# Rounding by conversion to int16, a clip moved to VectorE, separate priorities for the first and last batches, and a last batch without softmax transfers

## The chip, the cores and the metric

The kernel runs on one core of a Trainium2 chip. Its time is the device time of one execution in microseconds (us), and lower is better. The core has five engines that run side by side and meet at semaphores: TensorE (PE, matmuls, results in PSUM), VectorE (DVE), ScalarE (ACT), GpSimd (POOL) and SyncE (SP), whose queue issues all DMA transfers of this kernel.

## The reference

For each of 32 batches (x and context are 128 x 512 in f32): cross-attention over 8 heads, then a feed-forward network whose weights are ternary and whose activations are rounded to 8 bits per token.

```python
x = x + xattn(layernorm(x), ctx)      # 8 heads of 16 channels, rope on 8 of them, softmax over 512 keys
x = x + ffn(layernorm(x))

def act_quant(x):                     # per token
    scale = 128 / clip(max(abs(x)), 1e-5)
    return clip(round(x * scale), -128, 127) / scale

def weight_quant(w):                  # one scale for a whole matrix
    scale = 1 / clip(mean(abs(w)), 1e-5)
    return clip(round(w * scale), -1, 1) / scale

def ffn(x):                           # 512 -> 2048 -> 512
    gate, up = bitlinear(x, w_gate), bitlinear(x, w_up)
    return einsum(act_quant(fwht(silu(gate) * up)), weight_quant(w_down))
```

`fwht` is a Walsh-Hadamard transform over the 2048 channels.

## The kernel before

Every batch passes through some forty stages. Each stage is a Python generator (`s_load`, `s_a`, ..., `s_dn`) that loops over the batches and yields what it needs next: a buffer of a ring (`get`), an event of another stage (`on`), or an engine for a stated time. The class `Plan` runs all generators against a model of the engines and so writes down one fixed order of instructions for each engine. It takes the step that can start first by its model; among steps of the same engine that could start within `eps` of it, the one with the lowest rank goes first. A rank is the stage's number in `CFG` plus `T` times the batch index, as the stage last gave it with `at`; a stage without an `at` (the weight stages `w`, `w1` to `w4`, `const`, `init`) keeps its number. On TensorE `stick` is taken off the rank of a step whose matmul shape ("full", "half" or "cols") is that of the step before. `pen` keeps a step that two engines could do on the first named.

Attention of a batch: `s_load` fetches x and context; `s_a`, `s_a2`, `s_a3` normalise, project and apply rope, and write `xd` to DRAM; `s_st` reads it back as `qs` and `ks`. The 16 steps of `s_mpe` write scores to `pS` (two PSUM banks, one such buffer), `s_mdve` takes their row maxima `M` on VectorE (L657), `s_mfin` sends them back through DRAM into `qs`. `s_epe` repeats the scores into `pT` (also one buffer), `s_eact` takes the exponential on ScalarE (L725), and `s_eav` multiplies by the values, to which columns of ones are appended, so that `pav` holds the sums of the softmax too. `pS` and `pT` matmuls use half of the array's rows each ("half"). `s_u` copies `pav` to `U` (L769) and writes it to DRAM as `ud`. `s_o` reads from there the sums `sc` and the values `N`, inverts the sums (`rc`, L800), writes them out as `rd`, reads them back spread over 128 partitions as `RB`, and multiplies (L812). A matmul with `WOT` (L821) and an addition (L825) make `x1`.

Feed-forward: `s_o2` normalises `x1`, rounds it by adding 12582912 on ScalarE into a PSUM bank `w` (L854), subtracts that and clips at 127 on VectorE (L857) into `xq`, and a DMA transposes it to `xqT`. Gate and up projections (L880), silu (L910), product (L935), four rounds of butterflies (`s_bf`, L964, on GpSimd or VectorE) and two Hadamard matmuls (`s_hm`) fill `y`, 128 x 2048 in f32, of which there is one buffer. `s_am` finds each token's maximum, `s_q` scales (L1099), and `s_q1` and `s_q2` round and clip in two ScalarE passes over each half:

```python
nc.scalar.activation(y, y, AF.Identity, bias=MAG)                                  # s_q1, L1109
nc.scalar.activation(s["yq"][:, w], s["y"][:, w], AF.Relu, bias=MAG7, scale=-1.0)  # s_q2, L1123
nc.tensor.matmul(ps, s["yq"][:, j, :], WDQ[:, j, :], ...)                          # s_dn, L1141, 16 of them
nc.tensor.matmul(ps, NEG, CS, start=False, stop=True)                              # s_dn, L1142
```

The second pass holds 127 - y, so the down projection comes out as 127 times a column sum of the weights less what is wanted; one more matmul with `NEG` and the column sums `CS` takes that off, and `yc` carries the minus sign. `CS` is made once, in `s_w4`, with 16 matmuls (L418), four small VectorE steps and a transfer. `s_dn` then scales, adds `x1` (L1147) and writes the batch out.

At the start the three weight matrices are read in twelve pieces (`s_w`), summed by absolute value (`s_w1`), scaled, rounded, clipped and converted (`s_w2` to `s_w4`). The first gate matmul waits for all of them (`wr`, 2). The ring `pf` holds three PSUM banks that almost all full-array matmuls share, and `x1` has four buffers.

Of the kernel before, what the change touches and what calls it, by code (L numbers as in the profile page):

```python
# [13 lines left out]
F8 = mybir.dt.float8e4  # L14
AF = mybir.ActivationFunctionType
# [5 lines left out]
MAGIC = 12582912.0  # L21
# [4 lines left out]
    "a": 17040.0,  # L26
    "a2": 9587.6,
    "a3": 24145.2,
    "am": 15370.4,
    "bf": 32443.0,  # L30
    "const": -13702.6,
    "dn": -12954.6,
    "eact": -26357.5,
    "eav": 10024.8,
    "epe": -25661.6,
    "gact": 12255.9,
    "gpe": 25689.6,
    "hi": 17693.4,
    "hm": -13331.7,
    "init": -13147.7,  # L40
    "lo": 14260.1,
    "load": -14103.3,
    "mdve": -26910.2,
    "mfin": -15116.6,
    "mpe": -17532.8,
    "o": -16894.5,
    "o2": -35355.2,
    "q": 9579.7,
    "q1": 31393.3,
    "q2": 30321.2,  # L50
    "st": -39068.5,
    "u": 12892.7,
    "udve": -12899.7,
    "upe": 40468.8,
    "v": 41001.5,
    "w": 11036.2,
    "w1": 23901.9,
    "w2": 38371.3,
    "w3": 34207.9,
    "w4": 33907.2,  # L60
    "yv": -12466.7,
    "zt": 12210.4,
    "T": 69.4,
    "eps": 0.025,
    "pen": 8.4,
    "stick": 7462.1,
    "epspe": 0.214,
# [5 lines left out]
    "xq": 1, "xqT": 2, "pf": 3, "z0": 2, "z1": 1, "hl": 2, "y": 1, "yq": 2, "ot": 1,  # L73
# [3 lines left out]
class Plan:  # L77

# [16 lines left out]
    def __init__(self, nc, rings, cfg):  # L95
# [12 lines left out]
        self.locked = False  # L108
        self.tail = 0
# [11 lines left out]
    def step(self, t):  # L121
        self.now = max(t[1], t[7] + self.LAT[t[6]]) if t[6] else t[1]
        while True:
# [10 lines left out]
            t[0] = self.cfg[t[4]] + self.cfg["T"] * r[1]  # L134
# [45 lines left out]
    def run(self):  # L180
        for t in list(self.tasks):
            self.step(t)
        while True:
# [4 lines left out]
            for t in self.tasks:  # L188
# [5 lines left out]
                elif isinstance(r[0], tuple):  # L194
                    f = [(self.start(t, e), e, d) for e, d in zip(*r[:2])]
                    pen = self.cfg["pen"] if t[5] < self.tail else 0.0
# [29 lines left out]
def xattn_ffn(  # L226
# [41 lines left out]
    MAG7 = const.tile([128, 1], F32, name="MAG7")  # L268
    nc.vector.memset(MAG7, MAGIC + 127.0)
# [10 lines left out]
    CW = const.tile([128, 388], F32, name="CW")  # L280
    WQ, WK, WVT, BRP, MASK = CW[:, 0:128], CW[:, 128:256], CW[:, 256:384], CW[:, 384:386], CW[:, 386:387]
    NEGC = CW[:, 387:388]
    CM = const.tile([128, 386], F32, name="CM")
    EYE, WOT, HADF, BVO = CM[:, 0:128], CM[:, 128:256], CM[:, 256:384], CM[:, 384:386]
    ROPE = const.tile([128, 2, T], F32, name="ROPE")
    COS, SIN = ROPE[:, 0, :], ROPE[:, 1, :]
    HAD = const.tile([128, 128], FR, name="HAD")
    BO = const.tile([128, 1], F32, name="BO")
# [8 lines left out]
    ob = const.tile([128, 1], BF, name="ob")  # L297
    nc.vector.memset(ob, 1.0)
    NEG = const.tile([2, 128], BF, name="NEG")
    CS = const.tile([2, 512], BF, name="CS")  # L300

    p = Plan(nc, RINGS, CFG)
    p.tail = NB - 2
    st = [dict() for _ in range(NB)]
    NU = 2 * NB
    EARLY = 6

    def s_const():
# [6 lines left out]
        nc.scalar.copy(HAD, HADF)  # L315
        p.mark("had")
# [9 lines left out]
    def s_init():  # L326
        yield "on", "cw"
        yield "dve", 0.2
        nc.vector.tensor_scalar(NEG, ones[0:2, :], NEGC[0:2], None, ALU.mult)
        z = zeros[:, :, None].to_broadcast([128, 2, T])  # L330
        for i in range(4):
            yield ("dve", "pool"), (1.13, 1.4), "port"
            E[p.eng].tensor_scalar(kss[i], z, MASK, None, ALU.add)
            p.mark("ks", i)
# [69 lines left out]
    def s_w4():  # L404
# [8 lines left out]
        yield "get", "y"  # L413
        yield "get", "pf"
        yield "pe", 3.5
        pc = ps_f.tile([128, 512], F32, name="pf")
        for j in range(NI):
            nc.tensor.matmul(pc[0:1, :], ob, WDQ[:, j, :], start=(j == 0), stop=(j == NI - 1))  # L418
        yield "dve", 0.6
        w = fp.tile([128, 2048], F32, name="y")  # L420
        ca, cb = w[0:1, 0:512], w[0:1, 512:1024].bitcast(BF).rearrange("p (a f) -> p a f", a=2)
        nc.vector.tensor_scalar(ca, pc[0:1, :], 1.0 / 64.0, MAGIC, ALU.mult, ALU.add)
        yield "dve", 0.6, "port"
# [794 lines left out]
```

## Time and profile before

| | |
|---|---|
| three runs | 1440.73, 1450.44 (median), 1453.01 us |
| profiled execution | 1449.79 us, of which the span is 1447.9 us |
| mean granted TensorE clock | 0.95 |
| busy share of the span | TensorE 94%, VectorE 81%, ScalarE 82%, GpSimd 68% |
| first and last `U` copy (L769) | 82.5 and 1365.3 us |
| first and last `ot` (L1147) | 278.7 and 1444.3 us |
| DMA queue of the kernel | 137588 packets, 213.84 MB, 50.4% of 16 engines' span |

The span runs from the first to the last instruction. A busy share is the time in which an engine had an instruction at work; matmuls are pipelined, their ends are modelled, and a busy TensorE need not be at its peak. "L12" is line 12 of the kernel; names such as `pf<-hi,HAD` are the tile written and the tiles read. An arrow in the idle column names what ended the idle time.

### The profile page before, as it was taken

What the parts mean: (1) busy time and instruction counts of PE and PEld (TensorE: products, weight loads), DVE (VectorE), ACT (ScalarE), POOL (GpSimd) and SP (SyncE); (2) the same over time, 40 slices, a digit from 0 to 9 for tenths busy, and PEclk for the clock granted to TensorE, in tenths of its full rate; (3) what the DMA queues carried; (4) which work ended last, traced back from release to release, by engine and by line L of the source; (5) the groups of instructions that cost most, each with busy time, mean ns of one, the idle gap of its engine ahead of it and who ended that gap; (6) DMA issues with size and microseconds to landing.
All of it is one profiled execution on the core that took longest, in us unless ns stands there. A gap on an engine that the chain in (4) does not pass through costs nothing.

```text
span 1447.9 us, 21862 instructions
## 1 busy us (share of the span) xinstructions
PE 1354.9 (94%) x7448; PEld 529.9 (37%) x7448; DVE 1173.9 (81%) x1755; ACT 1192.3 (82%) x1575; POOL 990.2 (68%) x778
## 2 busy tenths in 40 slices
PE   3797799999999999999999999999999999999965
PEld 1222233333334343333334433334333434433322
DVE  2975878888888888888888888888889888886565
ACT  5778977888988888888888888888888888888743
POOL 3112319987777878877777787887777777777830
PEclk7567999999999999999999999999999999999986
DMA  8948745454456565555445556555544555321100
GB/s 284 294 145 270 220 110 159 145 145 117 150 157 173 166 175 166 155 151 149 118 153 161 170 170 174 167 153 147 144 129 149 163 170 155 94 72 43 41 26 14
DMA packets 137699, 215.23 MB, mean 149 GB/s; under 512 B 37618, under 2 KB 39924, under 8 KB 136564
## 3 DMA queue, kind: packets, MB, share of 16 engines
q1 hardware_dynamic: 137588, 213.84, 50.4%
q8 instruction: 59, 0.97, 0.3%
q14 instruction: 52, 0.43, 0.1%
HBM read 107.35 MB, written 93.85 MB: 139 GB/s over the span
## 4 chain that ended last, share of the span: by engine, by line
PE 77%; POOL 7%; DVE 6%; ACT 5%; DMA 3%; issue 2%; SPq 0%; POOLq 0%; ACTq 0%; DVEq 0%
PE pav L746 16%; PE pf L880 13%; PE pT L712 13%; PE pS L642 9%; PE pf L1141 8%; POOL z L964 4%; PE pf L472 4%; PE pf L984 4%; PE pf L1023 3%; ACT P L725 2%; PE pf L821 2%; PE pf L552 2%; PE pf L1024 2%; DVE M L657 2%; POOL N L812 1%
## 5 line engine op out<-in xcount | busy, mean ns | idle before, releaser
L964 POOL TENSOR_TENSOR z<-z 128x512 f32<-128x512 f32 x489 | 616.7, 1283 | 103.0 <-DVE z L935 60.7
L657 DVE TENSOR_REDUCE M<-pS 128x2 f32<-128x1024 f32 x488 | 595.1, 1219 | 90.6 <-PE pS L642 89.1
L725 ACT ACTIVATE P<-pT 128x1024 f32<-128x1024 f32 x512 | 523.0, 1022 | 145.6 <-PE pT L712 144.0
L746 PE MATMUL pav<-P,va 128*32 128x512 f32 x2048 | 281.8, 623 | 0.0
L712 PE MATMUL pT<-qs,ks 50*128 50x512 f32 x1024 | 260.1, 504 | 20.8 <-ACT P L725 18.7
L642 PE MATMUL pS<-ks,qs 48*128 48x512 f32 x976 | 227.5, 457 | 12.3 <-DVE M L657 7.5
L712 PEld LDWEIGHTS pT<-qs,ks 50*128 50x128 f32 x1024 | 97.8, 187 | 242.2 <-ACT P L725 144.0
L448 POOL TENSOR_TENSOR arstd<-arstd,MHALF 128x1 f32<-128x1 f32 x32 | 18.5, 579 | 195.6 <-DVE arstd L445 160.5
L880 PEld LDWEIGHTS <-xqT 128*128 128x128 bf16 x1024 | 91.8, 99 | 155.3 <-issue 83.2
L1099 POOL TENSOR_TENSOR y<-y,YB 128x1024 f32<-128x1024 f32 x60 | 140.9, 2369 | 9.0 <-ACT YB L1085 9.0
L1141 PE MATMUL pf<-WDQ,yq 128*128 128x512 fp8e4 x512 | 127.9, 396 | 16.3 <-ACT yq L1123 16.3
L1051 DVE TENSOR_REDUCE ya<-y 128x128 f32<-128x1024 f32 x64 | 127.3, 1989 | 12.9 <-ACT y L1038 12.6
L642 PEld LDWEIGHTS pS<-ks,qs 48*128 48x128 f32 x976 | 95.9, 190 | 112.8 <-issue 43.5
L880 PE MATMUL pf<-WGQ,xqT 128*128 128x512 fp8e4 x512 | 131.4, 382 | 0.9 <-DVE ot L1147 0.5
L880 PE MATMUL pf<-WUQ,xqT 128*128 128x512 fp8e4 x512 | 126.8, 381 | 0.5 <-DVE X L525 0.2
L935 DVE TENSOR_TENSOR z<-z,pf 128x512 f32<-128x512 f32 x128 | 84.3, 675 | 17.2 <-PE pf L880 13.7
L996 ACT CAST hi<-pf 128x512 fp32r<-128x512 f32 x128 | 74.1, 586 | 26.8 <-PE pf L984 26.7
L910 ACT ACTIVATE z<-pf,tk 128x512 f32<-128x512 f32 x128 | 84.1, 684 | 8.0 <-PE pf L880 4.7
L1007 DVE TENSOR_TENSOR lo<-pf,hi 128x512 fp32r<-128x512 f32 x128 | 85.5, 675 | 3.0 <-ACT hi L996 3.0
L1141 PEld LDWEIGHTS <-yq 128*128 128x128 bf16 x512 | 46.7, 101 | 99.3 <-ACT yq L1123 27.4
L984 PE MATMUL pf<-CM,z 128*128 128x128 f32 x512 | 82.2, 285 | 0.8 <-DVE z L964 0.4
L1038 ACT COPY y<-pf 128x512 f32<-128x512 f32 x128 | 71.7, 584 | 9.5 <-PE pf L1024 9.4
(118 smaller groups left out, 1780.0 us busy)
## 6 DMA issues: line engine op xcount, KB each, us to landing
xd<-X SPq DMA_DIRECT2D x128, 512.0 KB
qs<-xd SPq DMA_DIRECT2D x128, 192.0 KB
ks<-xd SPq DMA_DIRECT2D x128, 192.0 KB
ud<-U SPq DMA_DIRECT2D x64, 256.0 KB
xt<-x SPq DMA_DIRECT2D x32, 256.0 KB
ct<-cx SPq DMA_DIRECT2D x32, 256.0 KB
RR<-R SPq DMA_DIRECT2D x64, 128.0 KB
N<-ud SPq DMA_DIRECT2D x32, 256.0 KB
```

Of the source, the lines that this page charges most:

```text
L642: nc.tensor.matmul(ps[e], qs[w, t, bass.ts(qt, 128)], ks[w, t, :], start=True, stop=True)
L657: nc.vector.tensor_reduce(m, ps[2], AX.X, ALU.max)
L712: nc.tensor.matmul(ps[:, e], ks[w, t, bass.ts(kt, 128)], qs[w, t, :], start=True, stop=True)
L725: nc.scalar.activation(P, TQ[u, n], AF.Exp, scale=0.25)
L746: nc.tensor.matmul(av[32 * h : 32 * h + 32, :], va[:, kt, 4 * hf + h, :], P[:, e], start=(kt == 0), stop=(kt == 3),)
L880: nc.tensor.matmul(ps, xqT[:, k, :], W[:, k, bass.ts(c, 512)], start=(k == 0), stop=(k == 3))
L964: E[p.eng].tensor_tensor(ix(dv, k), ix(av, 0), ix(av, 1), o)
L984: nc.tensor.transpose(ps[:, i, :], st[b]["z"][:, bass.ts(4 * c + i, 128)], EYE)
L1007: nc.vector.tensor_tensor(t, F.pop(("z", b, c)), F["hi", b, c].bitcast(F32), ALU.subtract)
L1051: nc.vector.tensor_reduce(ya[:, h], s["y"][:, 8 * h : 8 * h + 8].rearrange("p j t -> p t j"), AX.X, ALU.max, apply_absolute_value=True,)
L1099: E[p.eng].tensor_tensor(y, y, st[b]["YB"].to_broadcast([128, 8, 128]), ALU.mult)
L1141: nc.tensor.matmul(ps, s["yq"][:, j, :], WDQ[:, j, :], start=(j == 0), stop=False)
```

## The change

x is rounded by ScalarE's conversion to int16 (`xi`, in SBUF) and clipped at 127 by VectorE into `xq`. y is converted to int16 by ScalarE (`yi`, a new buffer; `y` is released after that) and clipped into `yq` by VectorE. `yq` now holds y itself: the correction matmul, `NEG`, `CS` and the making of the column sums are gone, and the first down projection waits for `wr`, 2. Each stage has three numbers in `CFG`, the one with `.h` for batches below 4 and the one with `.z` for the last four; all numbers and the planner's constants have other values. In the last batch (`SHORT`) the division of the softmax is done on VectorE by a reciprocal of `pav`, a shuffle of partitions and a product, the output projection by two matmuls with a spread copy of the weight (`WOZ`), and the transpose of `xq` by matmuls with a unit matrix and a copy. Parts are left out below; most lines of `CFG` among them.

```diff
 CFG = {
...
-    "epe": -25661.6,
-    "gpe": 25689.6,
-    "load": -14103.3,
-    "mpe": -17532.8,
-    "o": -16894.5,
-    "o2": -35355.2,
-    "w": 11036.2,
-    "T": 69.4,
-    "eps": 0.025,
-    "pen": 8.4,
-    "stick": 7462.1,
...
+    "epe": -29108.4,
+    "gpe": 54531.7,
+    "gpe.z": 1547.0,
+    "load": 44634.2,
+    "load.h": -38799.1,
+    "mpe": -16692.5,
+    "mpe.h": -40256.1,
+    "mpe.z": -21815.0,
+    "o": -21945.0,
+    "o.z": 51451.2,
+    "o2.z": -36890.7,
+    "w": 57939.8,
+    "T": 848.2,
+    "eps": 0.104,
+    "pen": 30.7,
+    "stick": 4180.0,
...
-    "xq": 1, "xqT": 2, "pf": 3, "z0": 2, "z1": 1, "hl": 2, "y": 1, "yq": 2, "ot": 1,
+    "xq": 1, "xqT": 2, "pf": 3, "z0": 2, "z1": 1, "hl": 2, "y": 1, "yq": 2, "yi": 1, "ot": 1,
...
-            t[0] = self.cfg[t[4]] + self.cfg["T"] * r[1]
+            part = ".h" if r[1] < self.head else ".z" if r[1] >= self.tail else ""
+            t[0] = self.cfg.get(t[4] + part, self.cfg[t[4]]) + self.cfg["T"] * r[1]
...
-                    pen = self.cfg["pen"] if t[5] < self.tail else 0.0
+                    pen = self.cfg["pen"] if t[5] < self.tail + 2 else 0.0
...
+    WOZ = CM[:, 386:642]
...
+    EYEB = const.tile([128, 128], BF, name="EYEB")
...
-    ob = const.tile([128, 1], BF, name="ob")
-    nc.vector.memset(ob, 1.0)
-    NEG = const.tile([2, 128], BF, name="NEG")
-    CS = const.tile([2, 512], BF, name="CS")
...
-    p.tail = NB - 2
+    p.head = 4
+    p.tail = NB - 4
...
+    SHORT = (NB - 1,)
+    SWAP = [i % 16 + 16 for i in range(32)]
...
+        yield "act", 0.2
+        nc.scalar.copy(EYEB, EYE)
...
-        yield "get", "y"
-        yield "get", "pf"
-        yield "pe", 3.5
-        pc = ps_f.tile([128, 512], F32, name="pf")
-        for j in range(NI):
-            nc.tensor.matmul(pc[0:1, :], ob, WDQ[:, j, :], start=(j == 0), stop=(j == NI - 1))
...
-        nc.sync.dma_start(out=CS, in_=cb)
-        p.now = p.done
-        p.put("y")
-        p.mark("cs")
...
+            if b in SHORT:
+                yield "get", "RB"
+                yield "dve", 0.7
+                av = TQ.pop(u)
+                U = op.tile([128, T], F32, name="U", bufs=2)
+                nc.vector.reciprocal(U, av)
+                yield "dve", 0.8
+                RB = op.tile([128, T], F32, name="RB")
+                nc.vector.stream_shuffle(RB, U, SWAP)
+                yield "dve", 0.68
+                nc.vector.tensor_tensor(U, av, RB, ALU.mult)
+                p.put("pa")
+                p.put("RB")
+                st[b]["U", hf] = U
+                p.mark("ud", u)
+                continue
...
+    def add_x1(b, po, xr):
+        yield "dve", 0.66
+        x1 = x1p.tile([128, T], F32, name="x1")
+        nc.vector.scalar_tensor_tensor(x1, po, BO, xr, ALU.add, ALU.add)
+        p.put("pf")
+        p.put("xr")
+        st[b]["x1"] = x1
+        p.mark("x1", b)
...
+            if b in SHORT:
+                yield "dma", 0.73, 0.45, 1.2
+                xr = op.tile([128, T], F32, name="xr")
+                nc.sync.dma_start(out=xr, in_=x[b])
+                p.marks["xr", b] = p.done
+                if b == 0:
+                    yield "on", "bo"
+                yield "on", "ud", 2 * b + 1
+                yield "get", "x1"
+                yield "on", "xr", b
+                yield "get", "pf"
+                yield "pe", 1.88
+                po = ps_f.tile([128, 512], F32, name="pf")
+                for hf in range(2):
+                    nc.tensor.matmul(po, WOZ[:, bass.ts(hf, 128)], s["U", hf], start=(hf == 0), stop=(hf == 1))
+                p.put("U", 2)
+                yield from add_x1(b, po, xr)
+                continue
...
-            yield "get", "pf"
-            yield "act", 0.75
-            w = ps_f.tile([128, 512], F32, name="pf")
-            nc.scalar.activation(w, l2, AF.Identity, bias=MAG, scale=sx)
-            yield "dve", 0.6
+            yield "act", 0.65
+            xi = xp.tile([128, T], I16, name="xi", bufs=1)
+            nc.scalar.activation(xi, l2, AF.Identity, scale=sx)
+            p.put("l2")
+            yield "dve", 0.35, "port"
             xq = xp.tile([128, T], BF, name="xq", bufs=1)
-            nc.vector.tensor_scalar(xq, w, -MAGIC, 127.0, ALU.add, ALU.min)
-            p.put("pf")
-            p.put("l2")
+            nc.vector.tensor_scalar(xq, xi, 127.0, None, ALU.min)
             yield "get", "xqT"
-            yield "dma", 0.5, 1.23
-            xqT = fp.tile([128, 4, 128], BF, name="xqT", bufs=2)
+            if b in SHORT:
+                yield "get", "pf"
+                yield "pe", 0.4
+                pt = ps_f.tile([128, 4, 128], F32, name="pf")
+                for k in range(4):
+                    nc.tensor.matmul(pt[:, k, :], xq[:, bass.ts(k, 128)], EYEB, start=True, stop=True)
+                p.put("xq")
+                yield "act", 0.48
+                xqT = fp.tile([128, 4, 128], BF, name="xqT", bufs=2)
+                nc.scalar.copy(xqT, pt)
+                p.put("pf")
+            else:
+                yield "dma", 0.5, 1.23
+                xqT = fp.tile([128, 4, 128], BF, name="xqT", bufs=2)
+                nc.sync.dma_start_transpose(out=xqT, in_=xq)
+                p.now = p.done
+                p.put("xq")
             s["xqT"] = xqT
...
-            nc.vector.tensor_scalar(yc, yc, SW[:, 2:3], -1.0, ALU.mult, ALU.mult)
+            nc.vector.tensor_scalar(yc, yc, SW[:, 2:3], None, ALU.mult)
...
+                if hf == 0:
+                    yield "get", "yi"
                 yield "act", 1.05
-                y = st[b]["y"][:, 8 * hf : 8 * hf + 8]
-                nc.scalar.activation(y, y, AF.Identity, bias=MAG)
+                if hf == 0:
+                    st[b]["yi"] = fp.tile([128, NI, 128], I16, name="yi", bufs=RINGS["yi"])
+                w = slice(8 * hf, 8 * hf + 8)
+                nc.scalar.copy(st[b]["yi"][:, w], st[b]["y"][:, w])
                 p.mark("q1", b, hf)
+            p.put("y")
 
     def s_q2():
         for b in range(NB):
@@ -1116,13 +1221,13 @@
             yield "get", "yq"
             for hf in range(2):
                 yield "on", "q1", b, hf
-                yield "act", 1.05
+                yield "dve", 0.45, "port"
                 if hf == 0:
                     s["yq"] = fp.tile([128, NI, 128], BF, name="yq", bufs=RINGS["yq"])
                 w = slice(8 * hf, 8 * hf + 8)
-                nc.scalar.activation(s["yq"][:, w], s["y"][:, w], AF.Relu, bias=MAG7, scale=-1.0)
+                nc.vector.tensor_scalar(s["yq"][:, w], s["yi"][:, w], 127.0, None, ALU.min)
                 p.mark("yq", b, hf)
-            p.put("y")
+            p.put("yi")
...
-                yield "on", "cs"
+                yield "on", "wr", 2
             yield "get", "pf"
             ps = ps_f.tile([128, 512], F32, name="pf")
             for g in range(2):
                 if g:
                     yield "on", "yq", b, 1
-                yield "pe", 1.73 + 0.22 * g
+                yield "pe", 1.73
                 for j in range(8 * g, 8 * g + 8):
-                    nc.tensor.matmul(ps, s["yq"][:, j, :], WDQ[:, j, :], start=(j == 0), stop=False)
-            nc.tensor.matmul(ps, NEG, CS, start=False, stop=True)
+                    nc.tensor.matmul(ps, s["yq"][:, j, :], WDQ[:, j, :], start=(j == 0), stop=(j == NI - 1))
...
+    woz = np.zeros((2, 4, 32, 128), f)
+    woz[:, :, 0:16] = a["L0_xattn_Wo"].T.reshape(2, 4, 16, 128)
+    woz = woz.transpose(1, 2, 0, 3).reshape(128, 256)
+    r["cm"] = np.concatenate([np.eye(128, dtype=f), a["L0_xattn_Wo"].T, h, bvo, woz], 1)
```

## The prediction

> **What bounds the kernel now.** I read four views, in this order: the windows (busy time of each engine by stage), TensorE's timeline over one steady batch, the groups of instructions of ScalarE and VectorE, and the chain that ended last, for its end.
>
> The windows first. I cut them at events of the trace: the last weight conversion ends by 187 us, the first `ot` is at 278.7, the last `pS` matmul at 1316.6, the last `U` copy at 1365.3. The columns are length, busy us of TensorE, its weight load, VectorE, ScalarE and GpSimd, then granted clock, DMA share and GB/s.
>
> ```profile
> core 0: us, PE busy (x) PEld busy (x) DVE busy (x) ACT busy (x) POOL busy (x), PEclk, DMA share, GB/s
> 0.00:100.00 100.00, 66.72 (x254) 25.32 (x258) 61.21 (x105) 67.84 (x85) 26.35 (x28) 0.61 0.75 247
> 100.00:187.00 87.00, 69.30 (x352) 21.43 (x344) 61.48 (x88) 80.01 (x89) 20.77 (x19) 0.83 0.78 234
> 187.00:279.00 92.00, 89.18 (x486) 33.13 (x484) 69.65 (x102) 70.91 (x92) 62.70 (x51) 0.98 0.46 129
> 279.00:1317.00 1038.00, 1034.55 (x5945) 409.92 (x5942) 903.98 (x1331) 895.97 (x1205) 815.18 (x635) 1.00 0.52 149
> 1317.00:1366.00 49.00, 44.52 (x237) 17.35 (x236) 23.93 (x46) 41.39 (x57) 46.10 (x35) 1.00 0.12 37
> 1366.00:1448.00 82.00, 50.61 (x188) 22.79 (x186) 53.62 (x86) 36.22 (x51) 19.09 (x13) 0.78 0.09 28
> ```
>
> From 279 to 1317 TensorE is idle 3.5 us of 1038, at clock 1.00. Busy matmul time alone proves little, so I looked at how they follow each other:
>
> ```profile
> 803.20 0.38 PE L1142 MATMUL pf<-CS,NEG 2*128 2x512 bf16 x1
> 803.52 0.50 PE L712 MATMUL pT<-qs,ks 50*128 50x512 f32 x2
> ...
> 805.28 0.50 PE L712 MATMUL pT<-qs,ks 50*128 50x512 f32 x2
> 805.62 0.45 PE L642 MATMUL pS<-ks,qs 48*128 48x512 f32 x2
> 806.00 1.06 PE L746 MATMUL pav<-P,va 128*32 128x512 f32 x8
> 807.03 0.50 PE L712 MATMUL pT<-qs,ks 50*128 50x512 f32 x2
> 807.46 1.07 PE L746 MATMUL pav<-P,va 128*32 128x512 f32 x8
> ```
>
> Each matmul starts as the one before lets go, and one pattern of ScalarE (`X` L583, `U` L769, `y` L1038) returns from 799.90 to 840.03: a batch costs 40.13 us, set by what TensorE issues. In the same window VectorE is busy 904 / 1038 = 87%, ScalarE 86%, GpSimd 79%. What a change takes from ScalarE there is worth nothing directly. The timeline also prices a change of matmul shape. A pair pT, pS takes 806.00 - 805.28 = 0.72 us (0.67 at 809.04); pT alone takes 0.43. Two lone groups instead of a pair cost 2 x 0.43 - 0.67 = 0.19 us more.
>
> At the ends TensorE is not the bound: busy times clock is 66.7 x 0.61 + 69.3 x 0.83 = 98 of the first 187 us and 50.6 x 0.78 = 39 of the last 82.
>
> ```profile
> L1109 ACT ACTIVATE y<-y,MAG 128x1024 f32<-128x1024 f32 x64 | 72.7, 1138 | 5.1 <-DVE y L1099 2.6 <-POOL y L1099 2.5
> L1123 ACT ACTIVATE yq<-y,MAG 128x1024 bf16<-128x1024 f32 x64 | 72.6, 1138 | 0.2
> ```
>
> These are the two passes over y: 2.28 us of ScalarE a batch each. The last view is the chain, at the end:
>
> ```profile
> 1382.97 0.60 DVE N L812
> ...
> 1399.59 1.02 PE pf L880 x4
> ...
> 1412.38 1.05 ACT yq L1123
> ...
> 1427.00 1.18 ACT y L1038 x2
> ...
> 1437.94 5.98 PE pf L1141 x16
> ```
>
> After attention the path goes through batch 31's softmax division (L812), its gate matmuls (L880), batch 30's clip (L1123), then batch 31's `y` and its down matmuls. I sum against this execution, 1449.79 us, of which 1447.9 is span and 1.9 lies outside; the median of the three times is 1450.44, 0.65 above.
>
> **The change part by part.**
>
> *Correction matmul.* L1142 goes, 32 times. Its group shows 384 ns, but matmuls overlap: the next starts 803.52 - 803.20 = 0.32 us later, and that is the price. 29 of them lie before the tail: 29 x 0.32 = 9.3 us on the path. (Three in the tail are counted below.) The column sum L418 goes too: 16 matmuls from 190.13 to 193.67, 3.5 us, in a stretch that is already full; the two `pT` waits of ScalarE beside it (2.17, 3.37) say it is on the path. Its four VectorE steps (0.7 + 0.7 + 0.4 + 0.4) and the `CS` transfer at 197.4 precede the first down projection near 270 by far and are worth nothing. Sum -12.8.
>
> *Clip of y on VectorE.* ScalarE loses L1123, 2.28 us a batch; L1109 only changes its output type, taken at the same 1138 ns. No cover is needed: it is off the path. VectorE gains two `tensor_scalar` of 128x1024, int16 to bf16. No row shows that type. Nearest is the f32 clip L401, 128x2048 in 1219 ns, so 0.6 us at 1024; the upper bound is a one-result rate, as L657, 1219 ns. I take 0.6, so 1.2 us a batch. The Trainium skill, "VectorE: DVE Perf Modes" (the perf-mode tier table), gives 693 ns for 2048 elements of a 16-bit SBUF `tensor_scalar`; by it a clip would be an estimated 0.35 us and the batch 0.7, and the sum below would not change, since the clip is off the path. No row of this trace has such a 16-bit case. For x, L857 (682 ns from PSUM) becomes an SBUF op; the 1x512 SBUF rows L424/L426 took 0.41, so -0.27; `xi` is taken at the 0.80 of L841, also 512 to SBUF, against 0.77 of L854. VectorE: 904 / 1038 x 40.13 = 34.9 + 1.2 - 0.3 = 35.8 of 39.8 us, at the worst 37.1. It stays below TensorE, so 0; behind the clip in VectorE's queue stand the `M` reductions L657, each of which frees the only `pS`, and for them see the rivals. `y` is free one ScalarE pass earlier and `w` no longer holds one of three `pf` banks: this can only move the order.
>
> GpSimd may pay for it. While VectorE ran butterflies in the tail, GpSimd's L964 took 1.79 and 1.75 us (at 1368.01 and 1371.35), against a median of 1.28. So a clip can stretch a GpSimd op by about 0.5, three a batch: 1.5 us on an engine that has 8.6 us a batch free (21% of 40.13). I take 0. The skill speaks against the change here: "SBUF — State Buffer" (two separate sides) says that VectorE in a two-port mode locks a port pair that GpSimd needs, and the other waits for the whole instruction. By it GpSimd loses only as long as the three clips, an estimated 1 us a batch, and the forecast is the same.
>
> *Priorities, all batches.* Of TensorE's stages `epe` stays foremost and `mpe` goes from second to fourth, behind `o` and `mfin`; all values are redrawn and `stick` falls from 7462 to 4180. The period listed above has 14 pairs and 4 lone groups, so the best order saves 2 x 0.19 = 0.4 us a batch, and splitting two more pairs costs as much. Over the 28 batches from 187 to 1317 us that is -11 to +11; I take -2 for the bank and buffer that come free earlier.
>
> *Head.* Feed-forward waits for all weights (`wr`, 2), the last at 186.2; `x1` of batch 0 was there at 142.4. ScalarE does 12 x (2 x 1.25 + 2.09 + 2.0) = 79 us of weights work. It is busy 80 of 87 us from 100 to 187 and idle 32 of the first 100. What can be won is most of that idle time, -25. `load` moves to the front and the `w` transfers, without an "at", fall behind (11036 to 57939): batch 0 starts sooner, while its first transfers `xd` (7.86) and `ks` (4.86) no longer queue behind megabytes, but weights come later. If the weights slip by a quarter of their 44 us of loading (12.6 MB at 284 GB/s), +10. I take -8, inside these, as the ends are decided by order alone.
>
> *Last batch without transfers.* The last `pav` group starts at 1362.37 and ends at 1363.4; `U` is copied at 1365.3 behind the table load and gate of batch 30; ud, sc, N, rd, RB follow, each waiting, and `x1` starts at 1384.85, 21.4 us after. Now: reciprocal, shuffle, product, four matmul instructions instead of two, add. The reciprocal of 128x512 has no row: 128x32 takes 333 ns, 128x1 164, so by slope 0.164 + 511 x 5.45 ns = 2.95; at least 0.68, as other 512 ops from PSUM. Shuffle and product 0.68 each, matmuls 2 x 1.1, handovers 0.3: `x1` after 4.5 to 6.8. I take 6.8, 14.6 less. The transpose: `xq` ends 1393.07, gate starts 1399.59; 0.4 of matmul plus 0.59 of copy plus 0.3 instead of 6.5 saves 5. Together 20 on batch 31's own chain. But what is late next is `y`, one buffer: batch 30 fills it at 1395.6 and releases it with the clip's end at 1414.5, and batch 31's first matmul into it starts at 1421.3. So 7 of the 20 count. `y` is now released after L1109, at 1412.3: 2.2 more. The down matmuls of batch 31 need the first half of y only and start after pass, pass, clip, 3.4 us; now after pass and clip, 1.2 + 0.6: -1.6. L1142 goes, -0.3. These make 11.1, and what batches 29 and 30 save in the same way I leave out against VectorE's three new steps. I take -11; from 0 (if VectorE's three steps delay batch 30, whose `y` sets the end) to -22.
>
> Sum: -12.8 - 2 - 8 - 11 = -33.8; 1449.8 - 33.8 = 1416.
>
> **The rivals.**
>
> *Ends give more.* Head -25 and tail -20 with -12.8 and -2: 1390. For it: 89 us without full-rate work in the head and 43 in the tail. Against: both are chains of single buffers (`y`, `z1`) and ScalarE's 79 us, which no order removes.
>
> *Order gives nothing.* Only the removed matmuls and the last clip count: -12.8 and -1.9: 1435. For it: the saturated stretch is 72% of the span. Against: five transfers leave the end of the chain.
>
> *Slower: VectorE late with `M`.* With clips at 1.2 us each between the reductions, `pS` comes free late, pT and pS part, and each parted pair costs 0.19. Savings of 34 us are 34 / 32 / 0.19 = 5.6 more parted pairs a batch: from there it is slower. With 9 of the 14 parted the steady part costs 9 x 0.19 x 28 = 48, less the 2 I had counted for order, and the time is 1416 + 50 = 1466. For it: VectorE is already named in 13 waits of `pS`, 7.5 us. Against: those waits lie mostly outside the saturated stretch, where TensorE idles 3.5 us in all.
>
> *The change does not remove the work*, say the int16 path needs another pass: the diff shows none; no chance given.
>
> **How the numbers follow.** Forecast 0.62 (own range 1397 to 1433), ends give more 0.14, nothing from order 0.13, slower 0.11. A difference within 1% of 1450 (1436 to 1465) can't be told from none. Half of the third case and a fifth of the fourth fall in it, and some of the first beyond its range: faster 0.78, same 0.12, slower 0.10. The range goes from 1388, where half of the second case lies above, to 1447, which takes in the third: about 0.18 stays out.
>
> **What would show it.** Right: the steady pattern returns in 39.8 us or less; no L1142, L418, L1123; last `U` product within 7 us of the last `pav`; the first L880 before 187. Wrong: the period above 40.1 with more lone pT and pS groups; VectorE's clips at 1.2 us; the first gate after 190; the last `ot` more than 80 us after the last `pav`.

## The result, and the profile after

| | before | after |
|---|---|---|
| median of 20 runs each | 1444.51 us | 1452.12 us |
| ratio to before, 95% interval | | 1.0044, 1.0029 to 1.0059 |
| profiled span | 1447.9 us | 1450.2 us |
| last weight conversion, first gate matmul | 186.3, 187.2 us | 176.0, 177.2 us |
| first `ot` | 278.7 us | 250.3 us |
| steady batch (last `P` of batch 8 to that of batch 28, by 20) | 40.23 us | 41.05 us |
| batches 11 to 25 alone (last `P` of batch 10 to that of batch 25, by 15) | 40.31 us | 40.85 us |
| last `pav` ends; from there to the end | 1363.4; 84.5 us | 1372.8; 77.4 us |

The change made the kernel 0.3 to 0.6% slower, where 1416 us and at most 1447 were forecast. In these profiles both ends are shorter. The stretch between them is longer, by more than they won. The profiled execution of before took 1449.79 us, 5.3 above its median, and that of after is at its median, so the spans lie closer together than the medians.

Batches are numbered from 0. The 20 batches of the row "steady batch" are not all alike: in the order of after the exponentials of batches 26, 27 and 28 come 39.1, 45.2 and 41.7 us apart (40.1, 40.1 and 39.4 before). Where two orders are compared, the row of batches 11 to 25 is the one to go by.

The windows of the kernel after, cut at the same kind of events (last weight conversion, 279, 1317, last `pav`), with the columns that the prediction explains:

```profile
core 0: us, PE busy (x) PEld busy (x) DVE busy (x) ACT busy (x) POOL busy (x), PEclk, DMA share, GB/s
0.00:100.00 100.00, 63.47 (x292) 24.81 (x292) 66.27 (x108) 73.76 (x91) 26.40 (x28) 0.74 0.80 264
100.00:177.00 77.00, 62.14 (x298) 18.69 (x298) 53.45 (x75) 70.75 (x80) 20.93 (x16) 0.78 0.66 216
177.00:279.00 102.00, 99.44 (x566) 38.14 (x564) 82.48 (x118) 83.37 (x109) 63.53 (x51) 1.00 0.50 155
279.00:1317.00 1038.00, 1020.18 (x5802) 402.75 (x5800) 936.76 (x1358) 827.81 (x1132) 822.06 (x635) 1.00 0.49 146
1317.00:1373.00 56.00, 50.56 (x261) 20.04 (x260) 40.55 (x69) 41.91 (x58) 47.07 (x35) 0.94 0.13 39
1373.00:1450.00 77.00, 51.41 (x197) 25.30 (x195) 59.90 (x92) 27.31 (x44) 26.88 (x19) 0.77 0.04 14
```

From 279 to 1317 TensorE was idle 3.5 us before; now it is idle 17.8, and it starts 5802 matmuls in the same 1038 us where it started 5945; only 26 of the difference are correction matmuls. The clock is 1.00 in both. ScalarE lost 68 us of work there, as the change says, and VectorE gained 33: 90% of the window now, 87% before.

The groups of instructions that answer to L1109 and L1123 of before, with that of GpSimd's butterflies; the first line is the butterflies before:

```profile
L964 POOL TENSOR_TENSOR z<-z 128x512 f32<-128x512 f32 x489 | 616.7, 1283 | 103.0 <-DVE z L935 60.7
L1064 POOL TENSOR_TENSOR z<-z 128x512 f32<-128x512 f32 x493 | 630.8, 1303 | 47.6 <-DVE z L1035 32.6 <-DVE z L1064 5.3 <-PE pf L1246 0.7
L1228 DVE TENSOR_SCALAR yq<-yi 128x1024 bf16<-128x1024 int16 x64 | 69.1, 1106 | 1.4 <-ACT yi L1213 1.1
L1213 ACT CAST yi<-y 128x1024 int16<-128x1024 f32 x64 | 66.4, 1044 | 10.8 <-POOL y L1199 9.3 <-DVE y L1199 1.3
```

The clip L1228 has a mean of 1106 ns, but no clip is like the mean: they go from 410 to 1506 ns, with a median of 1192. Seven have no GpSimd operation beside them and take 414 to 428 ns. The other 57 take 1190 on the average, and their ends stand at a fixed distance from another event: 281 to 287 ns after the end of the GpSimd operation that ran when they started (10th to 90th percentile of the 55 that had one; the other two met one that started later). So the clip itself is short, and the rest of its length is a wait for GpSimd to finish. The butterflies, for their part, went only from 1283 to 1303 ns.

One place in a steady batch, in the timeline of the kernel after (start, length, instruction; the bracket is idle time before it and what ended it):

```profile
815.17 5.38 POOL L1064 TENSOR_TENSOR z<-z 128x512 f32<-128x512 f32 x4
...
815.66 1.23 DVE L710 TENSOR_REDUCE M<-pS 128x2 f32<-128x1024 f32 x1
...
816.79 2.62 DVE L1228 TENSOR_SCALAR yq<-yi 128x1024 bf16<-128x1024 int16 x2
...
817.65 0.41 PE L695 MATMUL pS<-ks,qs 48*128 48x512 f32 x2
...
819.34 1.21 DVE L710 TENSOR_REDUCE M<-pS 128x2 f32<-128x1024 f32 x1
...
820.60 0.51 PE L695 MATMUL pS<-ks,qs 48*128 48x512 f32 x2 [0.46 <-DVE M L710]
```

GpSimd works through four butterflies without a gap, so both clips wait. New scores are in `pS` at 818.06, but their maximum starts at 819.34, behind the clips in VectorE's queue. `pS` is one buffer, so the next scores wait for that maximum, and TensorE stands still. The same place is found 41 us earlier and 41 us later. In the view of TensorE's waits this is the line that grew, while that of `pT` did not. Before, then after (us in all, times, longest):

```profile
PE pS L642 <- DVE M L657: 7.5, 13, 1.6
PE pT L712 <- ACT P L725: 18.7, 25, 2.9
...
PE pS L695 <- DVE M L710: 18.6, 37, 1.4
PE pT L765 <- ACT P L778: 16.4, 24, 2.6
```

At the end, the chain of the kernel after (start, length, what):

```profile
1353.77 3.28 DVE U L823
...
1358.58 1.94 PE pav L799 x8
...
1372.84 3.37 DVE U L823
1376.24 0.73 DVE RB L826 x2
...
1381.35 0.67 DVE x L849
...
1393.14 3.41 PE pf L980 x8
...
1440.53 6.06 PE pf L1246 x16
```

`x1` of batch 31 starts 8.5 us after the last `pav` (21.4 before), its gate matmuls 11.8 after that (14.7 before). The reciprocal L823 is on the chain twice: the second time as foreseen, the first time because it holds the only `pav` buffer while TensorE wants to fill it again at 1358.58.

### The profile page after: what moved, and what is told of

Its sections match the earlier page's. It is cut to its first block, busy times and chain, and to the rows that moved or that the text cites. A ratio compares the mean times of both kernels' runs of the same rounds, so it can differ in the third digit from the quotient of the medians.

```text
span 1450.2 us, 21687 instructions
## 1 busy us (share of the span) xinstructions
PE 1347.2 (93%) x7406; PEld 529.7 (37%) x7406; DVE 1239.4 (85%) x1814; ACT 1124.9 (78%) x1511; POOL 1006.9 (69%) x782
## 4 chain that ended last, share of the span: by engine, by line
PE 67%; DVE 18%; ACT 8%; issue 4%; DMA 2%; SPq 0%; POOL 0%; DVEq 0%; ACTq 0%; POOLq 0%
PE pav L799 14%; PE pf L980 13%; PE pT L765 11%; PE pS L695 8%; PE pf L1246 7%; DVE M L710 7%; PE pf L1084 4%; ACT P L778 3%; PE pf L525 2%; DVE yq L1228 2%; DVE ya L1151 2%; PE pf L605 2%; PE pf L917 2%; DVE z L1035 2%; PE pf L1123 2%
## 5 line engine op out<-in xcount | busy, mean ns | idle before, releaser
L1064 POOL TENSOR_TENSOR z<-z 128x512 f32<-128x512 f32 x493 | 630.8, 1303 | 47.6 <-DVE z L1035 32.6
L765 PE MATMUL pT<-qs,ks 50*128 50x512 f32 x1024 | 257.7, 498 | 18.6 <-ACT P L778 16.4
L695 PE MATMUL pS<-ks,qs 48*128 48x512 f32 x976 | 226.0, 455 | 26.3 <-DVE M L710 18.6
L695 PEld LDWEIGHTS pS<-ks,qs 48*128 48x128 f32 x976 | 95.4, 190 | 127.3 <-DVE M L710 67.7
L908 POOL TENSOR_TENSOR N<-N,RB 128x512 f32<-128x512 f32 x30 | 38.6, 1285 | 102.6 <-DMA RB<-rd 52.8
L525 PE MATMUL pf<-ct,CW 128*32 128x512 f32 x256 | 79.2, 679 | 0.1
```

The lines of the kernel that those rows point to most:

```text
L695: nc.tensor.matmul(ps[e], qs[w, t, bass.ts(qt, 128)], ks[w, t, :], start=True, stop=True)
L765: nc.tensor.matmul(ps[:, e], ks[w, t, bass.ts(kt, 128)], qs[w, t, :], start=True, stop=True)
L1064: E[p.eng].tensor_tensor(ix(dv, k), ix(av, 0), ix(av, 1), o)
```

## The experiments

Three theories were open after these readings: the clip on VectorE waits for GpSimd and makes `M` late (A); the new order of the steady stretch is a worse one (B); the separate numbers of the last batches cost what the middle would have won (C). A change of the planner's numbers, or of a time that it is told, gives another order of the whole program. So most experiments keep the order of one of the two kernels as it is and exchange single instructions.

**The clip on another engine** (`clip_act`, `clip_pool`).

```diff
-                nc.vector.tensor_scalar(s["yq"][:, w], s["yi"][:, w], 127.0, None, ALU.min)
+                nc.scalar.copy(s["yq"][:, w], s["yi"][:, w])                                # clip_act
+                nc.gpsimd.tensor_scalar(s["yq"][:, w], s["yi"][:, w], 127.0, None, ALU.min) # clip_pool
```

> The changed kernel with the clip of y issued on ScalarE as a plain conversion from int16 to bf16; the clip at 127 of y is left out. The order of every other instruction on every engine is that of the changed kernel. Theory A (the clip on VectorE waits until the GpSimd operation beside it ends, 1.19 us instead of 0.42, the row maxima queue behind it and TensorE's pS comes late): a steady batch falls from 41.05 us to 40.3 to 40.5, the pS waits of 0.46 us disappear, time some 15 to 20 us below the changed kernel. Theory B (the redrawn order alone makes the batch longer, the clip's wait is hidden): the steady batch stays at 40.9 to 41.1 and the time within 4 us. ScalarE gets 2.1 us a batch at places that were not planned for it, which can take back up to 0.5 us a batch under either.

> The changed kernel with the clip of y issued on GpSimd, in the place that the order gives it; nothing is left out and all other orders are the same. Theory A: VectorE has no wait for GpSimd left in this step and the batch falls towards 40.4 us, unless GpSimd's own queue, which gets 2 x 1.2 to 2.4 us a batch more on 79% busy, becomes late for the butterflies (then above 41). Theory B: the batch stays at 41.0.

Measured: on ScalarE 1480.54 us, ratio 1.0232 (1.0203 to 1.0260), a steady batch of 41.96; on GpSimd 1595.98 us, ratio 1.1023 (1.0992 to 1.1055), a batch of 46.45. The copy on ScalarE leaves out the clip at 127. The groups of the two kernels:

```profile
L1228 ACT CAST yq<-yi 128x1024 bf16<-128x1024 int16 x64 | 66.8, 1050 | 0.1
```

```profile
L1228 POOL TENSOR_SCALAR yq<-yi 128x1024 bf16<-128x1024 int16 x64 | 176.6, 2773 | 23.5 <-ACT yi L1213 23.5
```

Neither engine can take the pass at this place of the order. On ScalarE the wait of `pS` for `M` falls from 18.6 to 11.9 us, but that of `pT` for `P` rises from 16.4 to 37.4: 2 x 1.05 us stand in front of exponentials, and TensorE needs those as much as it needs `M`. On GpSimd one clip takes 2773 ns, and the butterflies come late. So taking the clip away from VectorE removes one wait and puts a dearer one in its place; that VectorE's wait costs something is supported by the 11.9, its price is not.

**The clip without a wait, and no step at all** (`clip_free`, `clip_none`).

```diff
-                    st[b]["yi"] = fp.tile([128, NI, 128], I16, name="yi", bufs=RINGS["yi"])
+                    st[b]["yi"] = fp.tile([128, NI, 128], BF, name="yi", bufs=2)
-                nc.vector.tensor_scalar(s["yq"][:, w], s["yi"][:, w], 127.0, None, ALU.min)
+                nc.vector.tensor_reduce(s["yi"][:, 8 * hf, 0:1],       # clip_free; clip_none has no line here
+                    s["yi"][:, 8 * hf + 2 : 8 * hf + 4].rearrange("p a t -> p (a t)"), AX.X, ALU.max)
-                    nc.tensor.matmul(ps, s["yq"][:, j, :], WDQ[:, j, :], ...)
+                    nc.tensor.matmul(ps, s["yi"][:, j, :], WDQ[:, j, :], ...)
```

> The changed kernel with its clip of y replaced by a step on VectorE that costs about the same alone (a maximum over 128x256, 0.4 us) but has one SBUF input and no two-port copy, so that nothing of GpSimd's can hold it; ScalarE writes y as bf16 and the down matmuls read that. Left out: the rounding of y to integers and its clip. Every engine's order is that of the changed kernel. Theory A (the wait for GpSimd in the clip is what makes the steady batch longer): the step takes 0.4 us each time instead of 1.19, the steady batch falls from 41.05 to 40.4 us or less, the time by 15 to 22 us. Theory B (the order of the new numbers costs it): the batch stays above 40.8 and the time falls by less than 6 us.

> As the kernel with the free step, but without that step too: nothing on VectorE between ScalarE's y and the down matmuls. Left out: rounding and clip of y. If VectorE's load counts beyond its wait (904 to 937 us of 1038 were busy), it is another 3 us or more faster than with the free step; if only the wait counts, within 2 us of it.

Measured: 1435.86 us, ratio 0.9905 (0.9878 to 0.9933), and 1434.17 us, ratio 0.9905 (0.9876 to 0.9935); steady batches of 40.31 and 40.28 us. The group of `clip_free`, and its window:

```profile
L1226 DVE TENSOR_REDUCE yi<-yi 128x1 bf16<-128x256 bf16 x64 | 24.5, 411 | 1.7 <-ACT yi L1213 1.6
```

```profile
279.00:1317.00 1038.00, 1028.33 (x5882) 405.86 (x5881) 912.92 (x1380) 843.34 (x1151) 827.83 (x646) 1.00 0.49 147
```

With a step as long as a clip that meets no GpSimd operation, a batch costs 41.05 - 40.31 = 0.74 us less, 40.85 - 39.97 = 0.88 in batches 11 to 25. TensorE is idle 9.7 instead of 17.8 us, and its wait for `M` over the run is 10.1 instead of 18.6. Taking away that step as well gives nothing more (39.94 in batches 11 to 25). The second buffer of y is not what wins here: ScalarE's conversion L1213 never waited for a clip in the kernel after, and its idle time in the row above is put down to `y`. So VectorE's plain load for the clip is free, as the forecast said, and what costs is that the clip is 0.7 us longer when it is held. That is 14.3 us between the two profiled spans; the ratios to before, 1.0044 and 0.9905, put it at 1.4%, 20 us, with intervals of 0.15 and 0.28% on them.

**A clip of constant length that GpSimd doesn't hold** (`clip_acc`).

```diff
-                nc.vector.tensor_scalar(s["yq"][:, w], s["yi"][:, w], 127.0, None, ALU.min)
+                nc.vector.tensor_scalar(s["yq"][:, w], s["yi"][:, w], 127.0, None, ALU.min, ALU.max, accum_out=CLA)
```

> The order of after, with the clip of y kept on VectorE at its place, but told to write a running maximum beside its result as well, a form that computes one result a cycle: an estimated 1.1 to 1.2 us for 128x1024 (as L710, 1.21 for the same count), which would not have to wait for GpSimd. So about the mean length of the clip as it is (1106 ns), without its spread (410 to 1506). If only the mean length of the clip sets its price (theory: 0.7 us longer than the 0.41 us that cost nothing): steady batch 41.0, time 1450, as after. If it is the meeting with GpSimd's operations (the end tied to an end of GpSimd) that sets it: steady batch 40.3 to 40.6, time 1436 to 1442. If the new form is held by GpSimd as well, the clip takes over 1.5 us and the time is above 1455.

Measured: 1458.24 us, ratio 1.0094 (1.0071 to 1.0116), a steady batch of 41.09 us. The clip is now two instructions in the groups:

```profile
L1229 DVE TENSOR_SCALAR_CACHE_REDUCE yq<-yi 128x1024 bf16<-128x1024 int16 x64 | 77.6, 1212 | 3.0
L1229 DVE DVE_READ_ACCUMULATOR yq<-yi 128x1 f32 x64 | 5.3, 82 | 0.0
```

All 64 take 1160 to 1222 ns, beside GpSimd or not: this form isn't held. And in a batch it costs what the held one does (40.86 in batches 11 to 25). So nothing about the meeting as such matters, only how long VectorE is taken at this place: 0.41 us is free, 1.1 to 1.3 us cost some 0.88 us a batch, whatever fills them. In time it stands 0.5% above the kernel after; 4.6 of the 7.8 us between their spans lie behind the last `pav` (82.0 instead of 77.4 us to the end), and what holds it there was not taken further.

**Shorter GpSimd operations** (`pool_half`).

```diff
-                    E[p.eng].tensor_tensor(ix(dv, k), ix(av, 0), ix(av, 1), o)
+                    if p.eng == "pool":
+                        for x in (slice(0, m), slice(m, 2 * m)):            # m: half of the columns
+                            nc.gpsimd.tensor_tensor(c3(ix(dv, k), x), c3(ix(av, 0), x), c3(ix(av, 1), x), o)
+                    else:
+                        E[p.eng].tensor_tensor(ix(dv, k), ix(av, 0), ix(av, 1), o)
```

> The order of after; every GpSimd butterfly (L1064, 1303 ns) is issued as two of half the columns. If the clip's length is a wait for the end of the GpSimd operation that runs beside it, it follows that operation's length: the mean of the clips that have GpSimd beside them goes from 1190 to about 0.41 + 0.1 + half of a 0.7-us operation + 0.28, 0.8 to 0.95, and none takes above 1.2; VectorE gets some 0.5 us a batch of the 1.5 back. If the length comes from sharing the memory or from the data type, it stays at 1.19. The time says less: by the multiplication L1199 (128x1024 in 2375 ns, so some 0.2 us a started operation) the halves cost GpSimd 15 x 0.2 = 3 us a batch more, of 8 to 9 that it has free: 1440 to 1465.

Measured: 1468.68 us, ratio 1.0114 (1.0054 to 1.0175). The groups of this kernel:

```profile
L1068 POOL TENSOR_TENSOR z<-z 128x256 f32<-128x256 f32 x986 | 701.9, 745 | 43.2 <-DVE z L1035 31.9 <-DVE z L1070 3.5
...
L1234 DVE TENSOR_SCALAR yq<-yi 128x1024 bf16<-128x1024 int16 x64 | 58.7, 944 | 2.3 <-ACT yi L1219 2.2
```

The halves take 745 ns, and the clip's length follows them: the median goes from 1192 to 765, 54 of the 57 beside GpSimd stay under 1.2 us (30 of 57 in the kernel after), and their ends still stand 283 to 288 ns after a GpSimd end. The mean of the 57 is 1008, above the expected 0.95, because two clips waited for 5.6 and 6.7 us; the longer one is told of below. In batches 11 to 25 the shorter waits pay: 40.60 us a batch instead of 40.85, though GpSimd works 69 us more in all. Over the kernel the halves don't pay (41.16 in the row of 20 batches, where batch 27 takes 51.5 us instead of 45.2). This shows what the clip waits for; sharing of the memory or the data type would have left it at 1.19.

**The correction alone** (`before_nocorr`, in the order of before).

```diff
-                    nc.tensor.matmul(ps, s["yq"][:, j, :], WDQ[:, j, :], start=(j == 0), stop=False)
-            nc.tensor.matmul(ps, NEG, CS, start=False, stop=True)
+                    nc.tensor.matmul(ps, s["yq"][:, j, :], WDQ[:, j, :], start=(j == 0), stop=(j == NI - 1))
```

> The kernel before without its 32 correction matmuls L1142 (left out: the correction, so the sum over 127 - y stays in); the orders of everything else are those of before. The prediction priced them at 0.32 us each, 29 of them on the path: 9.3 us, some 10 with the tail, and the steady batch falls from 40.2 to 39.9 us. If TensorE's order waits for the other engines' orders, not for its own length: under 4 us and a batch of 40.1 or more.

Measured: 1440.85 us, ratio 0.9955 (0.9928 to 0.9982), so 3 to 10 us; a steady batch of 39.91 against 40.23. The 0.32 us of the forecast is met to the hundredth. It also gives the price of the order. `clip_free` has no correction either and its clip costs nothing, so in the steady part it differs from this kernel by the order and by what ScalarE and VectorE do for the rounding. In batches 11 to 25 that price is nothing: 39.97 us a batch in both, with 14.0 pairs and 4.0 lone half-array groups in both orders, though the new one changes the shape of the matmuls 43 instead of 42 times. So B fell for the steady batches, and the held clip is all that they lost: 0.88 us, less 0.34 for the correction, is the 0.54 between before and after. In the row of 20 batches `clip_free` needs 40.31 - 39.91 = 0.40 us a batch more, 8.1 us in all; 6.1 of them lie in batches 26 to 28, which have 8.7 lone groups each instead of 4.3.

**The last batches** (`no_z`, `no_short`, `tail_copy`).

```diff
-            part = ".h" if r[1] < self.head else ".z" if r[1] >= self.tail else ""
+            part = ".h" if r[1] < self.head else ""        # no_z
-    SHORT = (NB - 1,)
+    SHORT = ()                                             # no_short
-                nc.vector.reciprocal(U, av)
+                nc.vector.tensor_copy(U, av)               # tail_copy
```

> The changed kernel without the separate numbers for the last four batches; they take the middle numbers. Theory C (the numbers for the last batches hold attention back while feed-forward drains, and the time is lost there): batches 29 to 31 of the exponentials come 41 us apart instead of 44 to 48, the last exponential ends near 1350 instead of 1368, and the end comes 5 to 18 us earlier. Theory D (that work is only moved: what attention loses there feed-forward gains): the last exponential is earlier but the stretch after it grows by as much, and the time stays within 4 us.

> The changed kernel with the last batch's softmax through the transfers again, and its transpose by DMA. As the prediction counted it, the end is 11 us later. By the trace of the changed kernel, where the stretch from the last exponential to the end is 81.8 us against 86.8 before: 5 us later. If the y buffer of the batches in front sets the end, 0 to 2.

> The order of after; in the last batch the reciprocal of pav (L823, 3353 ns, twice) is a copy, so the division by the softmax's sums is left out there. If the reciprocal, which holds the only pav buffer in front of the second half, is what took the missing 4 of the 11 us from the last batch (7 won): last pav to the end falls by 2.7 (the second reciprocal) and last pav itself comes 2.7 earlier (the first), so the time falls by 3 to 5.5, to 1447 to 1449. If what is late next is batch 30's y, as in the forecast, the time falls by less than 1.5.

`no_z`: 1472.64 us, ratio 1.0171 (1.0144 to 1.0197). The separate numbers do stretch batches 27 to 29: 45.2, 41.7 and 43.7 us after, 40.8, 39.2 and 41.1 without. But without them the last two come 51 and 53 us apart (48 and 48 after), and from the last `pav` to the end it takes 95.4 instead of 77.4 us. So the end as a whole is not what the numbers lose, and C fell. The last batches are planned anew here, so 18 us (1.0171 against 1.0044) is the difference of two orders. `no_short`: 1467.52 us, ratio 1.0143 (1.0113 to 1.0172). With the transfers `x1` of batch 31 comes at 1409 instead of 1381, and from the last `pav` to the end it takes 90.5 instead of 77.4 us. This too has an order of its own for the last batches, so the 13 us are the size of the effect and not a clean price.

`tail_copy` keeps the order: 1445.20 us, ratio 0.9987 (0.9958 to 1.0016). The reciprocal of the kernel after, as the list of that line's instructions gives it (count, then ns least, median and most):

```profile
L823 DVE RECIPROCAL U<-pav x2: 3348/3353/3358, 1353.7 to 1372.8; 128x512 f32<-128x512 f32 x2
```

```profile
L823 DVE COPY U<-pav x2: 681/686/692, 1355.6 to 1369.9; 128x512 f32<-128x512 f32 x2
```

The second one gives back its 2.67 us behind the last `pav` (74.8 instead of 77.4 us to the end). The first gives back more. This profile was 2.2 us behind that of after when the last `P` of batch 28 ended (1231.3 and 1229.1), where the two kernels do not differ yet; from there to the last `pav` it takes 138.5 instead of 143.6 us, 5.1 less. In the kernel after TensorE waits 3.5 us for `pav` (0.9 in `tail_copy`), its granted clock is 0.5 for 6.8 us from 1356.7 on (1.00 there in `tail_copy`), and the group of `pav` matmuls at 1358.58 takes 1.94 us, as the next one does, where 1.07 is usual. Together 7.8 us, near the 8.2 between the ratios, and more than the expected 3 to 5.5. Batch 30's `y` hides none of it.

## Why the prediction was wrong

In the profiled executions the way from 1447.9 to 1450.2 us can be laid out by the place of the last `pav`. Counting TensorE's matmuls up to 279 us, each at its start-to-start time in the steady stretch of before, the kernel after is 13.3 us ahead of before and `clip_free` 11.2; not all of this comes from the change (see the head). The correction: 29 x 0.32 = 9.3. From these, the last `pav` of `clip_free` would end at 1363.4 - 11.2 - 9.3 = 1342.9; it ends at 1359.7, so the order and the first reciprocal cost 16.8. That of the kernel after would end at 1363.4 - 13.3 - 9.3 + 16.8 = 1357.6; it ends at 1372.8, so the held clip costs 15.2. Behind it 7.1 us are won.

**Correction** (forecast -9.3): right. **Column sum** (-3.5) and **head** (-8): won in part, and their size is open. They cannot be parted by the runs; together they were put at 11.5, and the two profiles give 13.3. But the granted clock of the first 100 us was 0.61 in the profile of before and 0.74 in that of after. `before_nocorr`, whose head is that of before with its column sum, was granted 0.74 as well, and by the same count it is 7.3 ahead of before. The kernel after is 6.0 ahead of it, and `tail_copy`, with the head of after, 3.0. So the runs leave 3 to 13 us. The first gate is at 177.2, before the 187 that the forecast named as its sign, but in `before_nocorr` the old head has it at 181.2.

**Clip of y on VectorE** (forecast 0): this is the step that failed: "It stays below TensorE, so 0". The load was even overestimated: 0.6 us a clip were taken, and an undisturbed one has 0.42 (the estimate of 0.35 beside it was too little). But the clip is held to 1.19 us, and then it is not the engine's load that decides. VectorE had 2.7 us of a batch to spare even with "at the worst 37.1", but its queue runs in order: a maximum that stands behind two clips starts late, the only `pS` stays full, and TensorE waits. In place of 0 the runs show 0.88 us in each of batches 11 to 25 and 15.2 us by the sum above, 20 by the ratios of `clip_free` and after. The sentence on GpSimd looked at the right pair of engines and took the wrong one for the loser ("a clip can stretch a GpSimd op by about 0.5"): GpSimd lost 20 ns an operation, VectorE 0.77 us a clip. The Trainium skill, "SBUF — State Buffer" (two separate sides), says that whichever of the two starts first has the port pair for its whole instruction and the other waits. Here GpSimd was the first for 55 of the 64 clips, with operations three times as long as the clip; the forecast drew on the page for one direction only. This trace agrees with it in the other: VectorE waits. How long the waiter takes behind the end, the page gives only for a DMA of GpSimd's that waits for VectorE, some 115 ns; no run here shows that case, and the clips end 281 to 287 ns behind.

The **slower rival** named this wait, clips of 1.2 us included, and had the point from which it decides in the wrong place. It counted parted pairs only, 5.6 a batch for no gain at all; in batches 11 to 25 none more were parted than before. The cost came instead as idle time of TensorE and fewer matmuls in the same time. So the forecast's price for what a late `M` costs was missing a term: the wait itself, in each batch again at the same place.

**Priorities** (forecast -2, bounds -11 to +11): mis-sized. Of the 16.8 above, the first reciprocal takes 5.1 by `tail_copy`; some 12 us are left, about the upper bound, but not where it was looked for. The bounds were made from parted pairs in every steady batch, and there the order costs nothing. TensorE's idle time puts about half of the loss at the two ends of the stretch: from 279 to 408 us it idles 3.2 us in `clip_free` and none in `before_nocorr`, from 1104 to 1317 5.0 and 2.6, and in between, in 696 us, 1.5 and 0.9. Where the rest lies, and which of the new numbers does it, was not run.

**Last batch** (forecast -11): right in kind, 7.1 won behind the last `pav`, and some 5 lost in front of it. The last product `U` ends 4.9 us after the last `pav`, inside the 7 that were named. The reciprocal, read off a slope as 2.95, takes 3.35, which is small; what was left out is that it comes twice and holds a buffer that is not doubled.

By the signs that the forecast listed it is refuted twice: the period is above 40.1, and the clips take 1.2 us. The lone groups that it expected with the longer period did not come in batches 11 to 25.

None of these kernels that computes all of the reference is faster than before. `clip_free` shows 0.7 to 1.2% to be had if y could be rounded and clipped without holding VectorE longer than some 0.4 us; the runs on ScalarE, on GpSimd and with the running maximum are three ways that don't do it in this order. Whether an order made for a clip of 1.2 us would, was not run.

## What to carry to other kernels

An engine with spare time is not free for a new step: look at what stands behind that step in its queue, and at whether the buffer it releases is a single one; if so, the length of that one instruction counts, not the engine's share. A short VectorE operation in a two-port form beside an engine that runs long GpSimd operations back to back should be priced at about one of these operations, not at its own length (here 1.19 us beside operations of 1.30, against 0.42). A mean over batches says something only if they are alike. And when a change brings a new order along, exchange single instructions in a fixed order to price its parts; whatever is planned anew mixes everything.

## What was not expected of the hardware

A waiting VectorE is nearly always let in at the first end, even between GpSimd operations that follow each other closely: in the kernel after all 55 clips that started beside a running operation end within 0.4 us of its end, and in 52 of these cases the next operation starts less than 0.1 us after it. But not always: in `pool_half` 2 of 56 were not let in and took 5.58 and 6.74 us. Both met a product on `y` and then half butterflies in a row. This is the longer one, with ten of them:

```profile
1173.70 4.67 POOL L1205 TENSOR_TENSOR y<-y,YB 128x1024 f32<-128x1024 f32 x2
...
1177.37 6.74 DVE L1234 TENSOR_SCALAR yq<-yi 128x1024 bf16<-128x1024 int16 x1
...
1178.33 7.04 POOL L1068 TENSOR_TENSOR z<-z 128x256 f32<-128x256 f32 x10
...
1184.16 1.46 PE L1252 MATMUL pf<-WDQ,yq 128*128 128x512 fp8e4 x3 [4.97 <-DVE yq L1234]
```

The clip ends 5.8 us after the first of the ten starts, about eight of them later (0.70 us each), and TensorE stood 4.97 us for it. Why these two were passed over, no run shows. With whole butterflies no clip of the kernel after took longer than 1.51 us. The clip of x, 128x512 from int16, behaves like that of y: 283 to 285 ns at its quickest, up to 1377 when GpSimd is beside it. It is held in `clip_free` too, so its price is not in the 0.88. And the clip of y with a running maximum takes 1160 to 1222 ns whatever GpSimd does.
